# A decoder layer with latent attention, cross attention and routed experts: the router taken four sequences at a time, and the first loads, the turned x1 and the seam put in another order

## The chip, the core and the metric

The kernel runs on one core of a Trainium2 chip. A core has five engines that work at the same time, each with its own queue: TensorE (PE: matrix products and transposes; its weight loads are shown as PEld), VectorE (DVE), ScalarE (ACT), GpSimd (POOL) and SyncE (SP, which only issues DMAs here). The metric is the device time of one launch in microseconds (us); lower is better.

## What is computed

There are 32 sequences of 256 tokens with 256 features, and for each a context of 120 tokens. All data are float32. Cut to what matters:

```python
x = layernorm(x + latent_attention(x))        # causal, 16 heads, 72 latents
x = layernorm(x + cross_attention(x, ctx))    # 16 heads of 64
x = layernorm(x + experts(x))

def experts(h):                               # 16 experts of width 512
    scores = softmax(h @ gate_w.T).transpose(0, 2, 1)      # b, expert, token
    topk_w, topk_idx = top_k(scores, 32)      # each expert takes 32 tokens of each sequence
    x_tok = h[topk_idx]
    eo = (gelu(x_tok @ Wg.T) * (x_tok @ Wu.T)) @ Wd.T * topk_w
    return scatter_add(eo, topk_idx) + shared(h)           # shared: one gated layer for all
```

The router is the line with `scores`: a product of each token's 256 features with 16 columns, a softmax over the 16, and later the 32 best tokens of each expert.

## The kernel before

**Stages.** A first part does both attentions and the router, a second the experts. In the first part a loop runs over rounds n = 0 to 31, and each round holds work of three sequences: the latent attention of sequence n, the cross attention of n - 1, and the end of the cross attention and the router of n - 2. In the second part the sequences fall in two parts of 16; in each, 16 experts (`Expert`) gather their tokens by index, and 8 pairs of sequences (`Shared`) go through the shared layer and are stored.

**Order of work.** `tc.manual_schedule(engines={PE})` around both parts means that PE's instructions stand in the order in which the Python program writes them. The other engines' order is made by a planner, which takes by priority what its own clock holds for ready; `urgent()` raises a priority. Once made, the order on each queue is fixed, and an instruction that waits holds back all behind it on its engine. DMAs are issued by SP, except a few at the start by ACT and the gathers and scatters by index, which POOL issues.

**A round.** It has four sections, one for each group of four heads (`scores(n, g, k)`, then `turn` of the group before, then `queries` of the next). `queries(s, g)` (L330) multiplies by wd_sb and also fetches, with four small DMAs of SP (L334), the last 8 of the 72 latents of each head out of the tile q8, which `query_rest` (L317) has computed for all 16 heads at once. The tile qT has two buffers. `weigh` and `weigh_rest` (L461, products of 32 columns put into quarters of the array) use the softmax. `latent_out` adds and normalises to x1; `cross_values`, `turn_x1` (the tile x1T), `cross_queries`, `cross_scores`, `cross_turn`, `cross_weigh` and `cross_out` are the cross attention; `cross_out` ends in x2. A layernorm is DVE work with one POOL instruction in the middle (L150, the reciprocal root).

**The router.** `turn_x2` turns x2 and stores it for the shared layer. `route` (L622) makes, for one sequence, four products with the turned x2 as the stationary side and gate_w's 16 columns as the moving side, the softmax (two exponentials on ACT), a copy of the 16 scores behind the 256 features of x2 on POOL (L646), and two DMAs: the rows of 272 numbers that the experts gather, and the rows they add to. `select` (L651) ranks the tokens of eight sequences on DVE, and `place` (L680) makes the indices.

**PSUM.** Products land in a ring of six banks (tag "r") and two banks (tag "l", cross scores).

**The start.** `first_weights` (L217) loads wd_w straight into the two packed places of wd_sb: 64 latents of each head by two DMAs of SP, the last 8 of each head by two DMAs of ACT, and the biases by small DMAs (L233: 16 of them). `load_weights` and `out_weights` (18 DMAs) follow the first section of round 0 in the program.

**The seam.** After the rounds, `first_section(32)` still runs for the last two sequences. Then the rest of the last cross attention is written by hand between stretches of the first experts' work: `feed_forward` is a generator, and `fill(n)` takes n stretches of it. Its first stretch loads the weights and rows of units 0 and 1 and turns unit 0's. An expert's rows have three buffers (tag "xe"). A unit's stretches are four pairs of gate and up products, then two halves of its down product; then its rows are scattered, and unit u + 2 is loaded.

Of the kernel before, what the change touches and what calls it, by code (L numbers as in the profile page):

```python
# [26 lines left out]
P = 128  # L27
# [5 lines left out]
def decoder_kernel(  # L33
# [45 lines left out]
    LR = L - LM  # L79
    QSCALE = 1.0 / float(C // H) ** 0.5  # L80
# [59 lines left out]
    def layernorm(pool, dst, r, name):  # L140

        mv = pool.tile([P, TC, 2], F32, tag="mv", bufs=2, name=f"mv_{name}")
        rstd = pool.tile([P, TC], F32, tag="rstd", bufs=2, name=f"rstd_{name}")
        with urgent():
            for t in range(TC):
                st = pool.tile([P, 6], F32, tag="st", bufs=2, name=f"st_{name}_{t}")
                nc.vector.bn_stats(st, r[:, t, :])
                nc.vector.bn_aggr(mv[:, t, :], st)
            nc.vector.tensor_scalar(rstd, mv[:, :, 1], EPS, None, ALU.add)  # L149
            nc.gpsimd.tensor_tensor(rstd, rstd, mhalf, ALU.pow)  # L150
            for t in range(TC):
                nc.vector.tensor_scalar(
                    dst[:, t, :],
                    r[:, t, :],
                    mv[:, t, 0:1],
                    rstd[:, t : t + 1],
                    ALU.subtract,
                    ALU.mult,
                )
# [51 lines left out]
    gw_sb = cw.tile([P, DC, E], F32, name="gw_sb")  # L211

    v_bufs = [wp.tile([P, TC, VW], F32, name=f"v_{k}") for k in range(2)]
    for vb in v_bufs:
        nc.gpsimd.memset(vb, 0.0)

    def first_weights():  # L217
        nc.sync.dma_start(out=lat_sb, in_=latent_w.rearrange("(c p) l -> p c l", p=P))
        nc.sync.dma_start(out=latb, in_=latent_b.unsqueeze(1))
        by_head = wd_w.rearrange("(c p) (h l) -> p c h l", p=P, l=L)  # L220
        for d in range(DC):
            nc.scalar.dma_start(
                out=wd_sb[:, d, H * LM :].rearrange("p (h l) -> p h l", l=LR),
                in_=by_head[:, d, :, LM:],
            )
        for d in range(DC):
            nc.sync.dma_start(
                out=wd_sb[:, d, : H * LM].rearrange("p (h l) -> p h l", l=LM),
                in_=by_head[:, d, :, 0:LM],
            )  # L230
        nc.sync.dma_start(out=wdb_sb, in_=wd_b)
        for h in range(H):
            nc.scalar.dma_start(  # L233
                out=wdbs[h * LR : (h + 1) * LR, ZC - 1 : ZC], in_=wd_b[LM:, h : h + 1]
            )

        for odd in range(2):
            nc.vector.tensor_scalar(
                wdbs[odd * LM : (odd + 1) * LM, 0 : H // 2],
                wdb_sb[0:LM, :].rearrange("l (c two) -> l c two", two=2)[:, :, odd],  # L240
                QSCALE,
                None,
                ALU.mult,
            )
        nc.vector.tensor_scalar(
            wdbs[:, ZC - 1 : ZC], wdbs[:, ZC - 1 : ZC], QSCALE, None, ALU.mult
        )
        nc.sync.dma_start(out=outb, in_=out_b.partition_broadcast(P))
# [5 lines left out]
    def out_weights():  # L254
# [3 lines left out]
        for odd in range(2):  # L258
            nc.sync.dma_start(
                out=ow_sb[odd * LM : (odd + 1) * LM, 0 : ZC - 1, :], in_=by_pair[odd, 0:LM]  # L260
            )
        for h in range(H):
# [11 lines left out]
    def load(s):  # L274
# [3 lines left out]
        nc.sync.dma_start(out=st["x"], in_=x[s].rearrange("(t p) d -> p t d", p=P))  # L278
        st["c"] = ap.tile([P, DC, S2], F32, tag="c", bufs=3, name=f"c_{s}")
# [47 lines left out]
    def queries(s, g):  # L327
# [4 lines left out]
        for j in range(HG):  # L332
            h = g * HG + j
            nc.sync.dma_start(  # L334
                out=qT[LM:L, j, :], in_=st["q8"][h * LR : (h + 1) * LR, :]
# [264 lines left out]
    def cross_out(s):  # L600
# [10 lines left out]

        st["x2"] = ap.tile([P, TC, XW], F32, tag="x2", name=f"x2_{st['nm']}")
        layernorm(ap, st["x2"][:, :, 0:C], r2, f"2_{st['nm']}")

    def turn_x2(s):
        st = states[s]
        st["x2T"] = ap.tile([P, DC, T], F32, tag="xnT", bufs=1, name=f"x2T_{st['nm']}")
        transposed(st["x2T"], st["x2"][:, :, 0:C], f"px2T_{st['nm']}")
        nc.sync.dma_start(out=x2ts[s // 2][:, :, s % 2, :], in_=st["x2T"])

    def route(s):

        st = states[s]
        nm = st["nm"]
        pg = bank("r", [P, TC, E], f"pg_{nm}")
        for t in range(TC):
            project(
                pg[:, t, :],
                [(st["x2T"][:, d, t * P : (t + 1) * P], gw_sb[:, d, :]) for d in range(DC)],
            )  # L630
        gmax = ap.tile([P, TC], F32, tag="gmax", name=f"gmax_{nm}")
        nc.vector.tensor_reduce(gmax, pg, AX.X, ALU.max, negate=True)
        ge = ap.tile([P, TC, E], F32, tag="gexp", name=f"gexp_{nm}")
        gsum = ap.tile([P, TC, 1], F32, tag="gsum", name=f"gsum_{nm}")
        for t in range(TC):
            nc.scalar.activation(
                ge[:, t, :],
                pg[:, t, :],
                AF.Exp,
                bias=gmax[:, t : t + 1],  # L640
                accum_out=gsum[:, t, :],
            )
        nc.vector.reciprocal(gsum, gsum)
        score = scs[s // BG][:, :, s % BG, :]
        nc.vector.tensor_tensor(score, ge, gsum.to_broadcast([P, TC, E]), ALU.mult)
        nc.gpsimd.tensor_copy(st["x2"][:, :, C:], score)  # L646
        nc.sync.dma_start(
            out=xrows[s // BQ][block_rows(s), :].rearrange("(t p) d -> p t d", p=P), in_=st["x2"]
        )
        nc.sync.dma_start(  # L650
            out=acc[s // BQ][block_rows(s), :].rearrange("(t p) d -> p t d", p=P),  # L651
            in_=st["x2"][:, :, 0:C],
        )
        states[s] = {}
# [36 lines left out]
    ats = {}  # L691

# [4 lines left out]


    def first_section(n):
# [11 lines left out]
        run(weigh_rest, n - 1)  # L711
        run(cross_weigh, n - 2, 4)
        run(latent_out, n - 1)
        run(load, n + 1)
        run(cross_out, n - 2)
        run(cross_values, n - 1, 0)
        run(cross_values, n - 1, 1)
        run(turn_x1, n - 1)
# [8 lines left out]
    with tc.manual_schedule(engines={mybir.EngineType.PE}):  # L727
        load(0)
        first_weights()
        turn_x(0)  # L730
# [4 lines left out]
        for n in range(B):  # L735
            first_section(n)
            if n == 0:
                load_weights([(wk_sb, wk)])
                out_weights()
                load_weights([(wv_sb, wv), (wq_sb, wq), (wo_sb, wo), (gw_sb, gate_w)])  # L740

            run(scores, n, 1, 0)
            run(scores, n, 1, 1)
            run(turn, n, 0, 0)
            run(turn, n, 0, 1)
            run(scores, n, 1, 2)
            run(turn, n, 0, 2)
            run(queries, n, 2)
            run(cross_scores, n - 1, 0, 1)
            run(turn_x2, n - 2)  # L750
            run(cross_turn, n - 1, 0, 0, 0)
            run(cross_turn, n - 1, 0, 0, 1)
            run(cross_keys, n, 0)
            run(route, n - 2)

            run(scores, n, 2, 0)
            run(scores, n, 2, 1)
            run(turn, n, 1, 0)
            run(turn, n, 1, 1)
            run(scores, n, 2, 2)  # L760
            run(turn, n, 1, 2)
            run(cross_turn, n - 1, 0, 1, 0)
            run(queries, n, 3)
            run(cross_turn, n - 1, 0, 1, 1)
            run(turn_x, n + 1)
            run(weigh, n, 0)
            run(weigh, n, 1)
            run(cross_weigh, n - 1, 0)
            run(cross_scores, n - 1, 4, 0)
            run(keys, n + 1)  # L770
            run(query_rest, n + 1)

            run(scores, n, 3, 0)
            run(scores, n, 3, 1)
            run(turn, n, 2, 0)
            run(turn, n, 2, 1)
            run(scores, n, 3, 2)
            run(turn, n, 2, 2)
            run(values, n + 1)
            run(queries, n + 1, 0)  # L780
            run(cross_scores, n - 1, 4, 1)
            run(cross_turn, n - 1, 4, 0, 0)
            run(cross_turn, n - 1, 4, 0, 1)
            run(cross_keys, n, 1)


            if n - 2 >= BG and (n - 2) % BG == 0:
                place((n - 2) // BG - 1)
            if n - 2 >= 0 and (n - 1) % BG == 0:
                select((n - 2) // BG)  # L790
# [83 lines left out]
    class Shared:  # L874
# [27 lines left out]
        def down(self):  # L902
            for i, back in enumerate(self.backs):
# [7 lines left out]
                nc.vector.tensor_tensor(back, po, back, ALU.add)  # L911
                layernorm(fp, back, back, f"3_{s}")
                nc.sync.dma_start(out=out[s].rearrange("(t p) d -> p t d", p=P), in_=back)
# [17 lines left out]
    def feed_forward():  # L931
# [5 lines left out]
        units[0].load()  # L937
        units[1].load()
# [19 lines left out]
    with tc.manual_schedule(engines={mybir.EngineType.PE}):  # L958
# [3 lines left out]
        route(last - 1)  # L962
# [21 lines left out]
        route(last)  # L984
# [58 lines left out]
```

## Time and profile before

| what | us |
|---|---|
| median of three runs | 3546.3 (3544.41 to 3547.76) |
| the profiled execution | 3547.01 |
| its span, first to last instruction | 3545.2 |
| first scores of round 0 on PE | 21.98 |
| output product of latent attention, round by round | every 76.9 |
| last output product of latent attention, its start | 2457.26 |
| last product of the experts, its start | 3531.08 |

TensorE's granted clock is 0.996 of full speed over the span. In the timeline, times are from the span's start. A group of matmuls is given with its start, its length, its shapes (stationary, moving) and a count; a float32 product shows as two instructions, a transpose as one. A matmul's length includes the time in which it drains, which overlaps the next one, so the distance from start to start says what it costs.

### The profile page before, as it was taken

What the parts mean: (1) busy time and instruction counts of PE and PEld (TensorE: products, weight loads), DVE (VectorE), ACT (ScalarE), POOL (GpSimd) and SP (SyncE); (2) the same over time, 40 slices, a digit from 0 to 9 for tenths busy, and PEclk for the clock granted to TensorE, in tenths of its full rate; (3) what the DMA queues carried; (4) which work ended last, traced back from release to release, by engine and by line L of the source; (5) the groups of instructions that cost most, each with busy time, mean ns of one, the idle gap of its engine ahead of it and who ended that gap; (6) DMA issues with size and microseconds to landing.
All of it is one profiled execution on the core that took longest, in us unless ns stands there. A gap on an engine that the chain in (4) does not pass through costs nothing.

```text
span 3545.2 us, 58568 instructions
## 1 busy us (share of the span) xinstructions
PE 3480.9 (98%) x21580; PEld 2651.5 (75%) x21580; DVE 1627.3 (46%) x3674; ACT 1516.2 (43%) x5576; POOL 1092.4 (31%) x1100
## 2 busy tenths in 40 slices
PE   8999999999999999999999999998999999999999
PEld 6888888888888888888888888886655665555665
DVE  3555555565555556555455655544322223212233
ACT  3555554455555455555445555544411111111111
POOL 2233332223332223333222333223344420344310
PEclk9999999999999999999999999999999999999999
DMA  3000000000000000000000000001355542455421
GB/s 90 14 19 19 17 17 19 21 16 22 16 17 16 19 20 18 21 17 17 16 22 17 20 19 17 17 15 67 88 125 122 124 127 66 92 124 122 103 82 54
DMA packets 144198, 164.47 MB, mean 46 GB/s; under 512 B 31272, under 2 KB 120104, under 8 KB 143912
## 3 DMA queue, kind: packets, MB, share of 16 engines
q1 hardware_dynamic: 114952, 125.96, 11.9%
q0 software_dynamic: 24576, 34.62, 5.6%
q8 instruction: 172, 2.82, 0.3%
q14 instruction: 114, 0.93, 0.1%
q10 hardware_dynamic: 4384, 0.13, 0.1%
HBM read 105.61 MB, written 50.86 MB: 44 GB/s over the span
## 4 chain that ended last, share of the span: by engine, by line
PE 97%; DVE 1%; DMA 1%; POOL 1%; issue 0%; ACT 0%; ACTq 0%; POOLq 0%; DVEq 0%
PE po L176 13%; PE pS L375 10%; PE pq L176 7%; PE pg L176 7%; PE pqx L176 7%; PE pd L176 6%; PE pu L176 6%; PE pz L440 5%; PE pT L420 5%; PE pL L547 4%; PE pxT L570 3%; PE pc L586 3%; PE pkx L176 3%; PE pu_s L176 3%; PE pg_s L176 3%; PE pfo L176 3%
## 5 line engine op out<-in xcount | busy, mean ns | idle before, releaser
L402 POOL TENSOR_TENSOR sm<-sm,rs 128x512 f32<-128x512 f32 x384 | 396.6, 1040 | 357.4 <-DVE rs L401 334.5
L402 POOL TENSOR_TENSOR xsm_x<-xsm_x,rs_x 128x480 f32<-128x480 f32 x256 | 252.5, 986 | 729.4 <-DVE rs_x L401 727.5
L394 ACT ACTIVATE sm<-sm,nmax 128x128 f32<-128x128 f32 (+1 forms) x1024 | 458.5, 456 | 32.4 <-DVE nmax L388 30.8
L394 ACT ACTIVATE xsm_x<-pL,nmax_x 128x120 f32<-128x120 f32 x1024 | 359.6, 375 | 126.1 <-DVE nmax_x L557 124.9
L375 PE MATMUL pS<-kT,qT 72*128 72x128 f32 (+1 forms) x2048 | 388.1, 333 | 10.1 <-DMA qT<-q 9.3
L150 POOL TENSOR_TENSOR rstd<-rstd,mhalf 128x2 f32<-128x2 f32 x96 | 66.7, 695 | 908.2 <-DVE rstd L149 908.1
L375 PEld LDWEIGHTS pS<-kT,qT 72*128 72x128 f32 x2048 | 299.3, 194 | 29.3 <-issue 9.6
L384 DVE TENSOR_TENSOR sm<-pS,mask 128x512 f32<-128x512 f32 x384 | 261.6, 681 | 104.9 <-PE pS L375 101.2
L866 POOL DMA_INDIRECT acc<-eo,offs x128 | 200.3, 1565 | 341.2 <-DVE eo L861 300.6
L176 PE MATMUL pq<-xT,wd_sb 128*128 128x256 f32 x1152 | 281.4, 385 | 1.9 <-DMA wd_sb<-in_wd_w_dram 1.9
L176 PE MATMUL pqx<-x1T,wq_sb 128*128 128x256 f32 x1024 | 240.3, 388 | 33.1 <-DVE x1T L170 33.1
L516 ACT COPY vx<-pvx 120x512 f32<-120x512 f32 x64 | 37.5, 586 | 541.3 <-PE pvx L176 541.3
L388 DVE TENSOR_REDUCE nmax<-sm 128x2 f32<-128x512 f32 (+1 forms) x384 | 257.6, 671 | 1.4
L176 PE MATMUL po<-ow_sb,zT 128*128 128x256 f32 x1152 | 257.2, 382 | 0.0
L176 PEld LDWEIGHTS po<-ow_sb,zT 128*128 128x128 f32 x1152 | 216.3, 190 | 40.2 <-DVE cxT L598 11.2
L928 DVE TENSOR_TENSOR hT<-gl,pu 128x512 f32<-128x512 f32 x128 | 87.9, 687 | 339.6 <-PE pu L176 258.4
L176 PEld LDWEIGHTS pqx<-x1T,wq_sb 128*128 128x128 f32 x1024 | 190.8, 191 | 68.0 <-DVE x1T L170 40.6
L176 PE MATMUL pg<-xeT,wg 128*128 128x512 f32 x512 | 240.8, 593 | 0.8 <-DVE xeT L842 0.8
L176 PE MATMUL pu<-xeT,wu 128*128 128x512 f32 x512 | 240.6, 592 | 0.0
L176 PEld LDWEIGHTS pq<-xT,wd_sb 128*128 128x128 f32 x1152 | 211.6, 193 | 29.0 <-DMA wd_sb<-in_wd_w_dram 3.3
L176 PE MATMUL pd<-wd,hT 128*128 128x256 f32 x1024 | 226.6, 379 | 0.0
L176 PE MATMUL po<-wo_sb,cxT 128*128 128x256 f32 x1024 | 226.2, 379 | 0.0
(123 smaller groups left out, 5900.7 us busy)
## 6 DMA issues: line engine op xcount, KB each, us to landing
wg<-in_wg_dram SPq DMA_DIRECT2D x32, 512.0 KB
wu<-in_wu_dram SPq DMA_DIRECT2D x32, 512.0 KB
wd<-in_wd_dram SPq DMA_DIRECT2D x32, 512.0 KB
rows<-x SPq DMA_DIRECT2D x32, 272.0 KB
x<-in_x_dram SPq DMA_DIRECT2D x32, 256.0 KB
qT<-q SPq DMA_DIRECT2D x512, 8.0 KB
acc<-x SPq DMA_DIRECT2D x32, 256.0 KB
x2t<-x2T SPq DMA_DIRECT2D x32, 256.0 KB
```

The costliest lines, as they stand in the source:

```text
L176: nc.tensor.matmul(acc, lhsT, rhs, start=(i == 0), stop=(i == n - 1))
L375: nc.tensor.matmul(pS[:, a, :], st["qT", g][:, j, t * P : (t + 1) * P], st["kT"][:, 0:width], start=True, stop=True,)
L384: nc.vector.tensor_tensor(sm, pS, m.unsqueeze(1).to_broadcast([P, n, width]), ALU.add)
L388: nc.vector.tensor_reduce(nmax, sm, AX.X, ALU.max, negate=True)
L394: nc.scalar.activation(dst[:, a, :], src[:, a, :], AF.Exp, bias=nmax[:, a : a + 1], accum_out=rs[:, a, :],)
L402: nc.gpsimd.tensor_tensor(dst, dst, rs.to_broadcast([P, n, width]), ALU.mult)
L420: nc.tensor.transpose(pT[:, j, :], block, ident)
L440: nc.tensor.matmul(pz[odd * LM : (odd + 1) * LM, a, k * P :], st["v"][:, k, 0:LM], moving(st, g, 2 * a + odd, k), start=(k == 0), stop=(k ...
L547: nc.tensor.matmul(pLs[odd][:, j, :], st["qxT", c0][rows, j, t * P : (t + 1) * P], st["kxT"][rows, c0 + j, :], start=True, stop=True,)
L570: nc.tensor.transpose(pT[:, j, :], st["xsm", c0, t, odd][:, j, :], ident)
L586: nc.tensor.matmul(pc[odd * DH : (odd + 1) * DH, a, :], st["vx"][:, 2 * (c0 + j0 + a) + odd, :], st["xpt", c0, odd][:, j0 + a, :], start=True,
L866: nc.gpsimd.indirect_dma_start(out=acc[b], out_offset=self.rows(b), in_=eo[:, k, :], in_offset=None, compute_op=ALU.add,)
```

## The change

Six edits, all in one step.

- **Router.** gate_w is kept with 32 columns, the upper 16 zero. The turned x2 of four sequences is collected in one tile x2T (one buffer). In rounds 6, 10, ... 30, `route(b)` multiplies with gate_w stationary and the turned x2 moving: each sequence has a quarter of the array's columns and of the 128 result partitions. DVE copies the result, `score(b)` turns it back with two transposes and does the softmax for four sequences: one exponential on ACT, more on DVE. The scores go straight from their tile to the last 16 columns of the rows with two DMAs. x2's own rows are stored by `cross_out`. `route` stands behind `weigh_rest` in the first section, `score` behind the second `cross_values`. Ranking and placing come one round later; block 7 is routed and scored at the seam.
- **x1.** `turn_x1` stands between the two halves of `cross_values` instead of behind both.
- **First loads.** wd_w comes as one contiguous DMA into ow_sb's place, and DVE (the last 8 latents, group 0) and POOL (groups 1 to 3) copy it into wd_sb. The last 8 latents are laid out with the head inside, so q8's rows of one head lie 16 partitions apart. The biases' small DMAs are one. In the preamble and round 0 SP's order is as written too: the first qT group before the second sequence, wk and the rest, out_w in two halves between the later groups.
- **Seam.** `feed_forward` yields after unit 0's load. The rest of `first_section(32)` (from cross_out on) is inside the hand-written seam, after that one stretch, and POOL's order is as written from there to the end of the kernel.
- **End.** The last sequence is added, normalised and stored in two halves of 128 tokens.
- `load` is split in two (x, context).

```diff
     def queries(s, g):
             nc.sync.dma_start(
-                out=qT[LM:L, j, :], in_=st["q8"][h * LR : (h + 1) * LR, :]
+                out=qT[LM:L, j, :], in_=st["q8"][h::H, :]
             )
...
     def first_weights():
+        raw = ow_sb.rearrange("p a b -> p (a b)").rearrange("p (c n) -> p c n", c=DC)
         nc.sync.dma_start(out=lat_sb, in_=latent_w.rearrange("(c p) l -> p c l", p=P))
-        nc.sync.dma_start(out=latb, in_=latent_b.unsqueeze(1))
+        nc.sync.dma_start(out=raw, in_=wd_w.rearrange("(c p) n -> p c n", p=P))
+        nc.scalar.dma_start(out=latb, in_=latent_b.unsqueeze(1))
+        nc.scalar.dma_start(
+            out=wdbs[:, ZC - 1 : ZC], in_=wd_b[LM:, :].rearrange("l h -> (l h)").unsqueeze(1)
+        )
+        nc.scalar.dma_start(out=wdb_sb, in_=wd_b)
+        by_head = raw.rearrange("p c (h l) -> p c h l", l=L)
+        def pack(copy, g):
+            at = slice(2 * g * P, 2 * (g + 1) * P)
+            copy(
+                wd_sb[:, :, at].rearrange("p c (h l) -> p c h l", l=LM),
+                by_head[:, :, g * HG : (g + 1) * HG, 0:LM],
+            )
         for d in range(DC):
-            nc.scalar.dma_start(
...
+            nc.vector.tensor_copy(
+                wd_sb[:, d, H * LM :].rearrange("p (l h) -> p l h", h=H),
+                by_head[:, d, :, LM:].rearrange("p h l -> p l h"),
+            )
...
+        pack(nc.vector.tensor_copy, 0)
...
+        for g in range(1, NG):
+            pack(nc.gpsimd.tensor_copy, g)
...
+    def route(b):
+        pg = bank("r", [P, T], f"pg_{b}")
+        for d in range(DC):
+            for i in range(BQ):
+                nc.tensor.matmul(
+                    pg[i * QW : (i + 1) * QW, :],
+                    gw_sb[:, d, :],
+                    blocks[b][:, d, i, :],
+                    start=(d == 0),
+                    stop=(d == DC - 1),
+                )
+        gT = ap.tile([P, T], F32, tag="gT", bufs=1, name=f"gT_{b}")
+        with urgent():
+            nc.vector.tensor_copy(gT, pg)
+        blocks[b] = gT
+
+    def score(b):
+        pg = bank("r", [P, TC * BQ, QW], f"pgT_{b}")
+        gT = blocks.pop(b)
         for t in range(TC):
...
+            nc.tensor.transpose(
+                pg[:, t * BQ : (t + 1) * BQ, :].rearrange("p i e -> p (i e)"),
+                gT[:, t * P : (t + 1) * P],
+                ident,
+            )
...
+        nc.scalar.activation(ge, ge, AF.Exp)
...
+            rows = xrows[b][:, C:].rearrange("(i t p) e -> t p i e", t=TC, p=P)
+            nc.sync.dma_start(out=rows[t], in_=sc)
...
+    def routed(n):
+        return 3 <= n < B and (n - 2) % BQ == 0
...
         run(weigh_rest, n - 1)
+        if routed(n):
+            route((n - 3) // BQ)
         run(cross_weigh, n - 2, 4)
         run(latent_out, n - 1)
-        run(load, n + 1)
+    def first_section_rest(n):
+        if n:
+            run(load, n + 1)
+            run(load_context, n + 1)
         run(cross_out, n - 2)
         run(cross_values, n - 1, 0)
+        run(turn_x1, n - 1)
         run(cross_values, n - 1, 1)
-        run(turn_x1, n - 1)
+        if routed(n):
+            score((n - 3) // BQ)
...
+    with tc.manual_schedule(engines={mybir.EngineType.PE, mybir.EngineType.SP}):
         load(0)
         first_weights()
+        load_context(0)
...
+        load(1)
+        load_context(1)
+        load_weights([(wk_sb, wk)])
+        attention_round(0)
+    with tc.manual_schedule(engines={mybir.EngineType.PE}):
+        for n in range(1, B):
+            attention_round(n)
         first_section(B)
...
         units[0].load()
+        yield
         units[1].load()
         units[0].turn()
         yield
...
-    with tc.manual_schedule(engines={mybir.EngineType.PE}):
+    with tc.manual_schedule(engines={mybir.EngineType.PE, mybir.EngineType.Pool}):
+        fill(1)
+        first_section_rest(B)
         cross_scores(last, 0, 1)
         turn_x2(last - 1)
         fill(2)
-        route(last - 1)
...
         turn_x2(last)
         fill(1)
-        route(last)
+        route(last // BQ)
+        fill(1)
+        score(last // BQ)
         fill(3)
```

## The prediction

> **What bounds the kernel now.** I read the page first (busy shares, the chain that ended last), then TensorE's own waits, then the timeline where those waits sit.
>
> ```profile
> PE 3480.9 (98%) x21580; PEld 2651.5 (75%) x21580; DVE 1627.3 (46%) x3674; ACT 1516.2 (43%) x5576; POOL 1092.4 (31%) x1100
> ...
> PE 97%; DVE 1%; DMA 1%; POOL 1%; issue 0%; ACT 0%; ACTq 0%; POOLq 0%; DVEq 0%
> ```
>
> TensorE (PE) is the chain. Time can only come from PE work removed, from PE's waits, and from stretches in which PE runs slowly. The waits of PE, in total us, times, longest:
>
> ```profile
> PE pqx L176 <- DVE x1T L170: 33.1, 32, 8.8
> PE pS L375 <- DMA qT<-q: 9.3, 2, 6.3
> PE pxT L570 <- POOL xsm_x L402: 4.2, 2, 2.3
> ```
>
> One short wait in each of 31 rounds, one long one at the seam between attention and experts, two at the start: these are the places of the change.
>
> **The router.** Timeline of PE; start, us, what:
>
> ```profile
> 142.92 2.81 PE L461 MATMUL pzr<-pt,v 128*32 128x256 f32 x64
> 145.66 1.95 PE L586 MATMUL pc<-xpt,vx 120*64 120x256 f32 x16
> ...
> 185.42 0.97 PE L176 MATMUL pg<-gw_sb,x2T 128*128 128x16 f32 x8
> 186.24 2.00 PE L375 MATMUL pS<-kT,qT 72*128 72x128 f32 x12
> 188.08 1.04 PE L420 MATMUL pT<-ident,sm 128*128 128x128 f32 x8
> ```
>
> Starts count, not durations (an end contains the drain). Routing one sequence: 186.24 - 185.42 = 0.82, and the scores behind it take 1.84 where the same twelve without a router in front take 1.76 (200.74 to 202.50): 0.90 each, 32 x 0.90 = 28.8 us. The new form has 16 passes of 32 columns by 256 for four sequences. Its nearest row is pzr, also 32 columns in four quarters: 64 passes, half of 256 and half of 128, in 145.66 - 142.92 = 2.74 us, so 2.74/48 = 0.057 per 256 and 0.91 for 16. The two score transposes cost 0.11 each (pT: eight in 0.88); I add 0.1 for the seams between forms. 8 x 1.23 = 9.8 us: **gain 19**. Bounds: if the quarters did not overlap, 16 x 0.215 (pq: eight of 256 in 1.72) makes 29.3 and a gain of -0.5; with no seams 20. I take the pzr row. Off PE, the route's copy has latent_out, cross_out and the values (over 16 us) before score needs it; score's reductions have until its bank comes round again, six banks later. 64-byte score rows, two DMAs a block, stand on SP between the context load and the next qT group (166.46 and 179.16: 12 us free), and nothing reads them before the experts. Without that gap one round in four would lose their issue, nearest row gw_sb's 2.53 us: at most 2 x 2.5 x 8 = 40. x2's two row stores only move up to where one of them stands already (165.99). The next block's x2T waits for route to have read the old one, which is a whole section earlier. Ranking and placing come a round later; their users are the experts.
>
> **The wait for x1T.** All engines of one round:
>
> ```profile
> 165.22 0.74 DVE L152 TENSOR_SCALAR x<-r,mv,rstd 128x256 f32<-128x256 f32 x2 [0.80 <-POOL rstd L150]
> ...
> 166.39 0.69 DVE L170 COPY x1T<-px1T 128x512 f32<-128x512 f32 x1 [0.43 <-PE px1T L166]
> ...
> 167.13 5.23 PE L176 MATMUL pqx<-x1T,wq_sb 128*128 128x256 f32 x23 [0.78 <-DVE x1T L170]
> ```
>
> The transposes begin at 165.75 and issue for 4 x 0.11, so PE could go on at 166.19 and goes on at 167.13: 0.94 lost. With one value half (1.72) behind them, px1T is ready at 166.39 - 1.72 = 164.67, x1 itself has been there since 159.06, and PE comes to the queries at 166.19 as before. What is late next is the DVE queue: between 164.42 and 165.22 it idles for POOL's rstd of x2, then normalises x2 until 165.96. If the copy stands in that gap, it ends at 165.4 and nothing is left of the wait; if it stands behind the normalisation, it ends about 166.65, the queries start at 166.67, and 0.48 is left. The order on DVE isn't in this trace. Ends 0.46 and 0.94 a round; by readiness in this trace the copy is first by half a microsecond, too little to trust a planner's clock, so I take 0.70: 31 x 0.70 = **22** (14 to 29).
>
> **The start.** Chain of waits, then SP's own waits:
>
> ```profile
> 14.98 6.86 DMA qT<-q
> ...
> 37.51 8.25 DMA qT<-q
> SPq L334 <- DMA wo_sb<-in_wo_dram: 3.1, 1, 3.1
> ```
>
> The first scores wait until 21.98 and the third group's until 45.90, because qT's small copies stand on SP behind weights: a DMA issue waits for an older one to finish, 18 out_w issues take 23.77 to 33.4, the four big loads follow. After the change wd_w comes as one contiguous load third on SP, issued about 2.2; x needed 3.9 to arrive, and 1.18 MB at the 300 to 416 GB/s of the densest slices takes 2.8 to 3.9 more: about 7.3. Two small DVE copies (0.25 each by the 0.21 to 0.29 of the v copies) lead to query_rest: four slow passes of 0.43, ACT 0.46, q8 near 10.3, against 14.96. Four qT issues at 0.62 and two to three us of landing: first scores near 15, saving 7. Behind them on SP come load 1, wk (used at 40.95) and the second qT group, then a half of out_w (used near 68) between the later groups; no qT group waits for a big load that is less than a group old. The packs on POOL (three of about 1 us, by the 1.04 of a 512-wide product) are through by 12, before the second queries. From the first scores to the end of the first key block before took 42.7 - 21.98 = 20.7, at a slow clock for most of it (pq eight in 3.43 against 1.72). I keep these 20.7: third scores at 35.7 instead of 45.9. The next group was then slow again until 52 (5.66 of work in 8.55), which no longer happens: 2.9. **Gain 13.** Here a rule stands against the row: the Trainium skill, "TensorE: Matmul & The Clock Gate", Part 1, has the array at full clock after about 3.4 us of activity and cold again after such a window of idleness. By it the scores would be warm soon after 18 and the 11.7 us of full-speed work between (2.62 + 1.72 + 2.62 + 1.32 + 1.72 + 1.74) would end near 30: gain 19. But the trace, broken by small waits, is slow until 38.5, so I take the row. Ends 7 (only the DMA order helps at one place) and 19.
>
> **The seam.** Timeline of all engines:
>
> ```profile
> 2482.73 0.73 POOL L150 TENSOR_TENSOR rstd<-rstd,mhalf 128x2 f32<-128x2 f32 x1
> 2483.49 0.73 DVE L152 TENSOR_SCALAR x<-r,mv,rstd 128x256 f32<-128x256 f32 x2 [9.36 <-POOL rstd L150]
> 2484.14 0.68 DVE L170 COPY x1T<-px1T 128x512 f32<-128x512 f32 x1
> ```
>
> The x1T copy is behind x2's normalisation on DVE, that behind rstd on POOL, and that behind gathers for three experts at 1.25 us each; mv was ready at 2474.1. PE starts again at 2484.88 instead of 2475.91, and the 24 query passes take 7.59 where a round shows 5.45. By hand only the first expert's four gathers go ahead; they follow rstd of x1 at 2467.3 and end at 2473, so rstd of x2 isn't held. The second expert's four stand behind the products of the second cross scores (2501.3 to 2503.6) and land by 2512, wanted at 2523; the next products on POOL are due at 2510. At most 0.5 is left, as in a round: 8.97 + 2.14 - 0.5 = 10.6. **What is late next:** POOL in written order puts rstd of the last x2, ready at 2542.1, ahead of expert 0's scatter, and unit 2's gathers after that. Scatter 7.5 us, four gathers 1.25 to 1.3 apart, 2.8 to land: the last rows at 2557.3, wanted at about 2555.9. That costs 1.4, no more clock. Seam: **gain 9** (5 to 11). The 5 us of waits at 2440 to 2448 are untouched.
>
> **The end.** The last sequence is added, normalised and stored in halves: one 256-wide chain instead of a 512-wide one (0.3 + 0.37 + 0.15 + 0.37 shorter) and half the store, unless the first half delays the second on DVE: 0 to 1.2, **0.7**.
>
> **Sum** against the profiled execution (3547.0, span 3545.2 plus 1.8): 19 + 22 + 13 + 9 + 0.7 = 63.7, so 3483.3; the median is 0.7 below the profiled one: 3483. Removed exponentials and POOL's score copy cover nothing and gain nothing.
>
> **Rivals.**
> Slower: the experts' gathers. Before, POOL issued 12 gathers before any scatter, a unit ahead; in written order those for unit u+2 come after scatter u. In a steady unit: scatter from 2646.72, gathers at 2654.20 to 2658.06, landing 2.8, so 2660.9, wanted at 2662.95: 2.0 us of slack, 30 units. Each us beyond costs 30; the change is slower from 2.0 + 63.7/30 = 4.1 us extra per unit (5 us would give 3573). Against it: the median landing is 2.8 with the same scatters ahead of it; for it, the longest was 6.4. Chance 0.05, a fifth of it within the 0.2% below.
> Small gain: x1T behind x2's normalisation (14), start only 7, seam 6, or quarters that drain against each other (router 10): 14 + 15 + 7 + 6 = 42, 3505. For it: only the written order of PE is certain. Chance 0.23.
> Large gain: copy in the gap (29), start by the rule (19), seam 11, router 20: 79, 3468. Chance 0.20.
> The forecast, 3474 to 3494: 0.51. The router not overlapping at all, 3503: 0.01.
>
> 0.2% (7 us) is about what a measurement of this kernel can tell from no change. Range 3464 to 3507. Faster 0.95, same 0.01, slower 0.04.
>
> **What would show it.** Right: one route of about 0.9 us per four sequences; pqx's wait under 0.5 in a round; first scores near 15 and third near 36; no 8.8 at the seam, a wait of 1 to 2 for the third expert's rows. Wrong: px waiting for gathers in every unit, pS waiting for qT inside rounds (its source rows now lie 16 partitions apart; slack about 3 us), a cold PE after 40 us.

## The result, and the profile after

| | before | after |
|---|---|---|
| median, us | 3545.8 (4 runs, 3544.41 to 3547.76) | 3494.85 (4 runs, 3492.36 to 3495.5) |
| ratio, 95% interval | | 0.9855 (0.9837 to 0.9872) |
| the profiled execution / its span | 3547.01 / 3545.2 | 3492.36 / 3490.2 |
| first scores on PE | 21.98 | 19.13 |
| third scores | 45.90 | 37.73 |
| first output product of latent attention | 78.61 | 67.34 |
| last one | 2457.26 | 2409.66 |
| last product of the experts | 3531.08 | 3475.89 |

The change saves 51.0 us between the medians and 55.0 between the two spans; the profiled execution of after was its fastest. The forecast was 63.7 between spans. The rows of the table cut the 55.0 into places: 11.3 before the first latent output product, 36.3 in the 31 rounds to the last one, 7.6 between that one and the last product of the experts, and -0.2 behind it.

The page of after, busy shares and the chain that ended last:

```profile
PE 3449.6 (99%) x21468; PEld 2617.0 (75%) x21468; DVE 1632.7 (47%) x3639; ACT 1499.0 (43%) x5456; POOL 1090.3 (31%) x1073
...
PE 94%; DVE 3%; issue 1%; POOL 1%; DMA 1%; SPq 0%; ACT 0%; POOLq 0%; DVEq 0%; ACTq 0%
```

PE is still the chain, and its busy time fell by 31.3. TensorE's waits in after (total us, times, longest):

```profile
PE pk L178 <- DVE xT L172: 7.4, 1, 7.4
PE pqx L178 <- DVE x1T L172: 6.3, 24, 0.3
PE pxT L585 <- POOL xsm_x L417: 4.2, 2, 2.3
PE pxT L168 <- DMA x<-in_x_dram: 4.0, 1, 4.0
PE px L898 <- DMA xe<-rows,offs: 2.9, 2, 2.6
PE pS L390 <- DMA qT<-q: 2.3, 1, 2.3
PE px1T L168 <- DVE x L154: 1.6, 1, 1.6
```

The 33.1 us of waits for x1T are 6.3, the 8.8 at the seam is gone, and qT costs 2.3 rather than 9.3. One wait has grown: the first keys wait 7.4 for xT, where before it was 0.8. Two are new: the third expert's transposes wait 2.9 for gathered rows, and in round 1 the transposes of x1 wait 1.6 for x1, since no cross_out stands ahead of them there.

A plain round in after, all engines (start, length, engine, line, operation):

```profile
153.44 0.60 PE L168 MATMUL px1T<-ident,x 128*128 128x128 f32 x4
...
154.62 0.74 DVE L154 TENSOR_SCALAR x<-r,mv,rstd 128x256 f32<-128x256 f32 x2 [0.80 <-POOL rstd L152]
...
155.27 0.69 DVE L172 COPY x1T<-px1T 128x512 f32<-128x512 f32 x1
...
156.01 2.21 PE L178 MATMUL pqx<-x1T,wq_sb 128*128 128x256 f32 x9 [0.26 <-DVE x1T L172]
```

The transposes are through by 154.1, DVE is idle for 0.80 while POOL makes rstd for x2, and yet the copy stands behind x2's normalisation. It was ready in time and queued too late.

A round with a router, PE only:

```profile
434.40 2.81 PE L476 MATMUL pzr<-pt,v 128*32 128x256 f32 x64
437.03 1.05 PE L650 MATMUL pg<-x2T,gw_sb 128*32 128x256 f32 x16
438.00 1.95 PE L601 MATMUL pc<-xpt,vx 120*64 120x256 f32 x16
...
458.53 0.38 PE L667 MATMUL pgT<-ident,gT 128*128 128x128 f32 x2
458.96 1.35 PE L178 MATMUL pqx<-x1T,wq_sb 128*128 128x256 f32 x5
```

Start to start, the router of four sequences takes 0.97. The two transposes of score stand where PE would otherwise wait for x1T, so here they cost nothing: from one latent output product to the next it is 76.38 with a router in between and 75.52 without, 0.86 apart. (The experiment a2 below has no such wait, and there the transposes add 0.22 to the stretch behind.)

The start in after, all engines:

```profile
9.77 0.88 DVE L242 COPY wd_sb<-ow_sb 128x128 f32<-128x128 f32 x2 [1.26 <-DMA ow_sb<-in_wd_w_dram]
...
10.57 0.84 DVE L236 COPY wd_sb<-ow_sb 128x512 f32<-128x512 f32 x1
...
11.77 0.68 DVE L172 COPY xT<-pxT 128x512 f32<-128x512 f32 x1
...
12.50 1.98 PE L178 MATMUL pk<-xT,lat_sb 128*72 128x256 f32 x4 [7.38 <-DVE xT L172]
...
16.72 2.58 SPq L349 DMA_DIRECT2D qT<-q  x4
...
19.13 0.49 PE L390 MATMUL pS<-kT,qT 72*128 72x128 f32 x2 [0.43 <-ACT qT L363]
```

The copy of the turned x needs only PE's four transposes of x, which begin at 4.04 and have ended by 5.13, but it stands on DVE behind the copies into wd_sb, the first of which waits for wd_w until 9.77. So the keys start at 12.50, and q8 is fetched from 16.72: later than before, not sooner.

### The profile page after: what moved, and what is told of

It is laid out like the page before. It is cut to its first block, busy times and chain, and to the rows that moved or that the text cites. A ratio compares the mean times of both kernels' runs of the same rounds, so it can differ in the third digit from the quotient of the medians.

```text
span 3490.2 us, 58138 instructions
## 1 busy us (share of the span) xinstructions
PE 3449.6 (99%) x21468; PEld 2617.0 (75%) x21468; DVE 1632.7 (47%) x3639; ACT 1499.0 (43%) x5456; POOL 1090.3 (31%) x1073
## 4 chain that ended last, share of the span: by engine, by line
PE 94%; DVE 3%; issue 1%; POOL 1%; DMA 1%; SPq 0%; ACT 0%; POOLq 0%; DVEq 0%; ACTq 0%
PE po L178 13%; PE pS L390 10%; PE pq L178 7%; PE pqx L178 7%; PE pd L178 6%; PE pg L178 6%; PE pu L178 6%; PE pz L455 5%; PE pT L435 5%; PE pL L562 4%; PE pxT L585 3%; PE pc L601 3%; PE pkx L178 3%; PE pu_s L178 3%; PE pg_s L178 3%; PE pfo L178 3%
## 5 line engine op out<-in xcount | busy, mean ns | idle before, releaser
L390 PE MATMUL pS<-kT,qT 72*128 72x128 f32 (+1 forms) x2048 | 380.4, 329 | 3.3 <-DMA qT<-q 2.3
L152 POOL TENSOR_TENSOR rstd<-rstd,mhalf 128x2 f32<-128x2 f32 (+1 forms) x97 | 67.2, 693 | 935.4 <-DVE rstd L151 935.4
```

The costliest lines, as they stand in the source:

```text
L390: nc.tensor.matmul(pS[:, a, :], st["qT", g][:, j, t * P : (t + 1) * P], st["kT"][:, 0:width], start=True, stop=True,)
```

## The experiments

Each kernel is after with the edit shown, unless said otherwise; differences are between medians, against 3494.85 for after. Beside the experiments before measured 3546.42 to 3546.7, beside after 3545.83, so a difference of 1 us says nothing.

**Both value halves ahead of x1's transposes (a1).**

```diff
         run(cross_values, n - 1, 0)
-        run(turn_x1, n - 1)
         run(cross_values, n - 1, 1)
+        run(turn_x1, n - 1)
```

> The changed kernel with turn_x1 behind both halves of the values, as before. If the split of the values is what shortened the wait, each of 30 rounds loses 0.94 on PE again instead of 0.41, less about 0.4 in the 7 rounds where score's transposes lie in the wait: 14 to 17 us slower than the changed kernel. Rival (the rounds became shorter by the router alone): no difference beyond 3 us.

Measured: 3509.98 (3507.36 to 3510.87), 15.1 slower than after. The wait is back:

```profile
PE pqx L178 <- DVE x1T L172: 23.6, 32, 0.8
```

So this part of the change is worth about 15 us: a plain round is 76.04, 0.52 longer, and the 31 rounds together take 16.6 more.

**x1T copied by ACT (a2).**

```diff
-        transposed(st["x1T"], st["x1"], f"px1T_{st['nm']}")
+        transposed(st["x1T"], st["x1"], f"px1T_{st['nm']}", nc.scalar.copy)
```

> The changed kernel with the copy of x1T out of PSUM on ACT instead of DVE. Theory: what is left of the wait (0.41 a round) is the place of the copy on DVE behind x2's normalisation. ACT has only the values' copies there, so the wait should vanish in all rounds: about 24 x 0.41 = 10 us faster than the changed kernel, PE's list without pqx. Rival (the transposes themselves come too late, or x1 is late): the wait stays and the time with it, within 2 us.

Measured: 3479.05 (3478.43 to 3480.7), 15.8 faster than after; a plain round is 74.99. All engines of the same stretch:

```profile
153.55 1.88 PE L178 MATMUL pvx<-wv_sb,c 128*120 128x512 f32 x4
...
153.80 0.59 ACT L172 COPY x1T<-px1T 128x512 f32<-128x512 f32 x1
154.30 0.74 DVE L154 TENSOR_SCALAR x<-r,mv,rstd 128x256 f32<-128x256 f32 x2 [0.80 <-POOL rstd L152]
...
155.27 2.97 PE L178 MATMUL pqx<-x1T,wq_sb 128*128 128x256 f32 x13
```

With the copy on an engine whose queue is free, the queries follow the second value half without a wait. The direction was expected, the size missed: I had reckoned 0.41 a round, from start to start, and nothing in routed rounds. A plain round gains 0.53; the seven stretches behind a router gain 0.31, because the transposes of score, which the wait had hidden, now show. That is 13.5 over the 31 rounds; the profiled spans lie 12.9 apart, the medians 15.8 (after's profile is its fastest execution). In plain rounds, a1, after and a2 together show a wait of 1.05, of which the change takes one half and the copy on ACT the other.

**One router per sequence again (a3).** `route(s)` as it was in before (products with the turned x2 stationary), with all other parts of the change kept.

> The changed kernel with the router's product and softmax per sequence again (16 moving columns, at its old place in the round and at the seam), all else as changed. Theory: 0.90 a sequence against about 0.95 for four, so 28.8 - 7.6 = 21 us slower than the changed kernel, and 2 to 3 more because score's transposes no longer lie inside pqx's wait in 7 rounds. Rival (the quarters run one behind the other, so the new form costs the same): within 3 us.

Measured: 3516.55 (3513.2 to 3517.38), 21.7 slower. A round is 76.42 long. A plain one of after is 75.52, so one sequence's router costs 0.90, as the timeline of before had said; four in quarters cost 0.86 together. The 2 to 3 us more that I expected for the transposes of score did not show.

**xT first on DVE (a4).** DVE's order, too, as written in the preamble, with turn_x(0) and keys(0) ahead of the copies that wait for wd_w.

```diff
-    with tc.manual_schedule(engines={mybir.EngineType.PE, mybir.EngineType.SP}):
+    with tc.manual_schedule(
+        engines={mybir.EngineType.PE, mybir.EngineType.SP, mybir.EngineType.DVE}
+    ):
         load(0)
         first_weights()
         load_context(0)
-        turn_x(0)
-        keys(0)
+    with tc.manual_schedule(engines={mybir.EngineType.PE, mybir.EngineType.SP}):
         query_rest(0)
...
     def first_weights():
...
+        turn_x(0)
+        keys(0)
         by_head = raw.rearrange("p c (h l) -> p c h l", l=L)
```

> The changed kernel with DVE's order at the very start as written: the copy of xT ahead of the copies that wait for wd_w. Theory: keys and query_rest waited for xT until 12.5 only because that copy stood behind them on DVE; now keys are done before wd_w lands at 9.7, q8 is ready near 13 instead of 16.7, first scores near 16: 3 to 4 us faster than the changed kernel. Rival (wd_w's landing and the slow clock alone set the start): under 1 us.

Measured: 3490.6 (3488.52 to 3492.83), 4.3 faster than after. PE in a4:

```profile
5.87 1.98 PE L178 MATMUL pk<-xT,lat_sb 128*72 128x256 f32 x4 [0.79 <-DVE xT L172]
...
14.92 0.49 PE L392 MATMUL pS<-kT,qT 72*128 72x128 f32 x2 [0.43 <-ACT qT L365]
```

The keys start at 5.87 instead of 12.50, q8 is fetched from 12.26, and the first scores are at 14.92.

**SP's order by the planner (b3).**

```diff
-    with tc.manual_schedule(engines={mybir.EngineType.PE, mybir.EngineType.SP}):
+    with tc.manual_schedule(engines={mybir.EngineType.PE}):
```

> The changed kernel with SP's order in the preamble and round 0 left to the planner: the second sequence's x and context, wk and half of out_w ahead of the first qT group. Theory: 1.4 MB more compete with wd_w's load, and the first q8 comes later by their transfer: 3 to 5 us slower than the changed kernel, first scores near 22 instead of 19. Rival (with the one contiguous load, SP's order no longer matters): within 1 us.

Measured: 3493.35 (3491.74 to 3495.39), no different from after. The theory that SP's hand-written order brings the start's gain fell: first scores at 18.89, and the first latent output product even 2.3 earlier (65.02).

**Weights written where they stood before (c1).** As b3, and wk, out_w, wv, wq, wo and gate_w again between the first section of round 0 and the rest, loads of the next sequence ahead of them as before. wd_w stays one contiguous load.

> The changed kernel with SP's order left to the planner and the weight loads written where they stood before, all behind round 0's first section; wd_w still comes as one load. Theory: with the hand order gone the start lost nothing (b3), so the gain at the start comes from where out_w and the big loads are written; here the third qT group stands behind all of them again, the third scores begin at 43 or later instead of 35 to 38: 6 to 9 us slower than the changed kernel. Rival (the one contiguous load of wd_w is the gain): within 2 us.

Measured: 3502.26 (3501.62 to 3503.42), 7.4 slower than after. SP's timeline in c1:

```profile
24.94 4.96 SPq L276 DMA_DIRECT2D ow_sb<-in_out_w_dram  x8
29.94 0.40 SPq L265 DMA_DIRECT2D wv_sb<-in_wv_dram  x1
...
32.01 2.02 SPq L265 DMA_DIRECT2D gw_sb<-in_gate_w_dram  x1
34.15 8.08 SPq L349 DMA_DIRECT2D qT<-q  x8
```

and PE's in the same kernel:

```profile
41.66 3.75 PE L390 MATMUL pS<-kT,qT 72*128 72x128 f32 x12 [8.20 <-DMA qT<-q]
```

The third group's qT stands behind out_w and the big loads again. PE waits 8.20 for it (before waited 3.0 at this place, because its PE came there later), the third scores begin at 41.66 instead of 37.73, and they take 3.75 instead of 1.93, at a granted clock of 0.50. Against b3, which has the same planner's order on SP, the time is 8.9 longer. So where the weights stand in the program is what gains at the start.

**The old small loads in the new order (c2).** wd_w in two packed pieces by SP and two by ACT, the biases one by one, q8 with a head's 8 rows side by side; SP's order as in after.

> The changed kernel with wd_w and the biases loaded as before, straight into their places (4096 pieces of 256 bytes and 4096 of 32, 16 small bias loads), q8's rows of a head side by side; SP's hand order stays. Theory: before, q8 was ready at 14.96, now at 16.7, so the one load gains nothing: within 2 us of the changed kernel, first scores near 19. Rival: 4 us or more slower.

Measured: 3494.69 (3493.89 to 3495.47): no difference. PE in c2:

```profile
13.40 2.62 PE L178 MATMUL pq<-xT,wd_sb 128*128 128x256 f32 x6 [2.85 <-DMA wd_sb<-in_wd_w_dram]
```

In after, the contiguous load gains nothing: part of the query passes wait for wd_w until 13.40 in c2, and in after the xT copy keeps all of them until 14.28. But c2 belongs beside a4 too. Both have their keys early (at 5.60 and 5.87); with the small loads the first scores are at 18.10, with the contiguous one at 14.92, and the medians are 4.1 apart. So the contiguous load gains once the xT copy is out of its way. The rows 16 partitions apart cost nothing in the rounds: a plain one is 75.52 in c2 as in after.

**POOL's order at the seam by the planner (b1).**

```diff
-    with tc.manual_schedule(engines={mybir.EngineType.PE, mybir.EngineType.Pool}):
+    with tc.manual_schedule(engines={mybir.EngineType.PE}):
```

> The changed kernel with POOL's order at the seam left to the planner, which puts eight more gathers ahead of rstd of the second last x2 and all later gathers a unit ahead. Theory: rstd waits 8 x 1.25 = 10 us more, x1T behind it, so PE waits about 9 at the seam and runs cold for the queries after it (2), while the wait for the third expert's rows (3.4) goes: 6 to 9 us slower than the changed kernel. Rival (the seam's gain came from the stretches' new order alone): within 2 us.

Measured: 3500.68 (3497.23 to 3501.1), 5.8 slower (the spans of the profiled executions: 9.0). All engines in b1:

```profile
2435.33 0.95 POOL L889 DMA_INDIRECT xe<-rows,offs  x1 [0.30 <-issue]
2436.29 0.74 POOL L152 TENSOR_TENSOR rstd<-rstd,mhalf 128x2 f32<-128x2 f32 x1
2437.06 0.73 DVE L154 TENSOR_SCALAR x<-r,mv,rstd 128x256 f32<-128x256 f32 x2 [9.36 <-POOL rstd L152]
2437.71 0.68 DVE L172 COPY x1T<-px1T 128x512 f32<-128x512 f32 x1
...
2438.45 7.90 PE L178 MATMUL pqx<-x1T,wq_sb 128*128 128x256 f32 x24 [8.83 <-DVE x1T L172]
```

The gathers of three experts stand ahead of rstd again, the x1T copy behind both, and the 24 query passes run at a granted clock of 0.68. The same place in after:

```profile
2427.40 0.73 DVE L154 TENSOR_SCALAR x<-r,mv,rstd 128x256 f32<-128x256 f32 x2 [0.85 <-POOL rstd L152]
2428.05 0.68 DVE L172 COPY x1T<-px1T 128x512 f32<-128x512 f32 x1
...
2428.79 3.50 PE L178 MATMUL pqx<-x1T,wq_sb 128*128 128x256 f32 x15 [0.31 <-DVE x1T L172]
```

**The gathers of unit u + 2 ahead of unit u's scatter (b2).** `Expert.load` is split: `fetch()` issues the gathers.

```diff
         units[0].load()
+        units[0].fetch()
...
                 units[u + 1].turn()
+            if u + 2 < len(units):
+                units[u + 2].fetch()
             yield
```

> The changed kernel with the gathers of unit u + 2 written ahead of unit u's down product, so ahead of its scatter on POOL. Theory: the one wait of PE for gathered rows (2.9 us of waits, 3.4 from start to start) goes and nothing else changes: 3 us faster than the changed kernel. Rival (every unit lost something to the late gathers): 10 us or more.

Measured: 3488.96 (3488.13 to 3489.35), 5.9 faster than after; between the profiled spans 3.3 (3486.9 against 3490.2). The wait for the third expert's rows is gone. Of after, POOL and PE at this place (first POOL's timeline, a scatter of unit 0 and the last gather of unit 2; then PE's):

```profile
2484.00 1.78 POOL L929 DMA_INDIRECT acc<-eo,offs  x1 [0.20 <-issue]
...
2495.53 0.95 POOL L889 DMA_INDIRECT xe<-rows,offs  x1 [0.30 <-issue]
```

```profile
2497.38 0.33 PE L898 MATMUL px<-ident,xe 128*128 128x128 f32 x1 [0.28 <-DMA xe<-rows,offs]
2500.33 0.77 PE L898 MATMUL px<-ident,xe 128*128 128x128 f32 x5 [2.63 <-DMA xe<-rows,offs]
```

The last gather is issued at 2495.53 and its rows are used at 2500.33, 4.8 later; the two waits sum to 2.9, and against the same transposes without a wait the place is 3.4 longer. The rest of the 5.9 isn't explained by a row: the runs of after lie 3.1 apart, and its profile is the fastest of them. In c3, which is like after at this place, the wait of 2.43 is followed by a slow stretch that after's profile does not have (last section). The other executions of after may have had one; they left no trace.

**The last sequence stored whole (c3, a single run).** `parts = [slice(0, TC)]` for every sequence.

> The changed kernel with the last sequence stored whole. From the start of the last product to the end of the span it was 14.12 before and 14.31 changed. Theory: the halves stand one behind the other on DVE and give nothing: 14.1 to 14.2. Rival: 14.8 or more.

Measured: 3495.17, span 3492.7. From the last product of the experts to the end of the span it takes 14.1, with halves 14.3, before 14.1. The halves gain nothing: both halves' additions stand on DVE at 3482.99, behind the normalisation of the sequence ahead.

**The repairs together (b4).** a2, a4 and b2, and in the last first_section the softmax's use (`weigh`, `weigh_rest`) ahead of the two cross_turns that wait there for POOL.

> Four edits together on the changed kernel: x1T's copy on ACT, xT's copy first on DVE, gathers ahead of the scatter, and in the last first_section weigh and weigh_rest ahead of the two cross_turns that wait for POOL. If the parts add up: 15.8 + 4.2 + 3 and 4 to 6 for the last, about 3467. If they cover one another: above 3475.

Measured: 3463.85 (3462.08 to 3466.3), ratio to before 0.9769 (0.9756 to 0.9782): 31.0 faster than after, faster than both kernels. The chain that ended last in b4:

```profile
PE 99%; DVE 0%; ACT 0%; DMA 0%; POOL 0%; issue 0%; POOLq 0%; SPq 0%; ACTq 0%; DVEq 0%
```

a2, a4 and b2 gave 15.8 + 4.3 + 5.9 = 26.0, so about 5 are left for the last section, whose two waits of together 4.2 on POOL's products are gone. That edit was not run alone; the 5 is a difference of medians.

**b4 with SP's order by the planner (c4).**

> The four edits of b4 and SP's order left to the planner. Theory: in b3 the planner's order had the first output product 2.2 earlier (65.09 against 67.34), lost again at the seam by chance of the profile: 0 to 2 us faster than b4, about 3462. Rival (the hand order is worth something once q8 comes earlier): 2 us or more slower than b4.

Measured: 3470.38 (3467.86 to 3470.88), 6.5 slower than b4. SP's timeline in c4:

```profile
13.27 0.76 SPq L273 DMA_DIRECT2D ow_sb<-in_out_w_dram  x1
14.14 5.00 SPq L351 DMA_DIRECT2D qT<-q  x8
```

and PE's:

```profile
18.85 5.46 PE L392 MATMUL pS<-kT,qT 72*128 72x128 f32 x16 [3.25 <-DMA qT<-q]
```

In b4 the first scores start at 15.56. Here a part of out_w goes ahead of qT just when q8 is ready (qT is issued at 12.19 in b4), and PE waits 3.25. The sixteen passes then take 5.46, and the granted clock is 0.50 from 20 to 34, where b4 has 0.86 from 20 to 26 and 1.00 behind; why the slow stretch is longer here isn't shown. My expectation missed. In b3 the same part of out_w goes at 11.76, and q8 is ready only for a fetch at 16.57, so there it holds up nothing. Once DVE's order is mended, SP's hand order is worth 6.5.

## Why the prediction was right, and where its sizes were off

The measured median is inside the range of 3464 to 3507, and 0.9 above the middle band of 3474 to 3494. Router, x1T, start and seam moved for the reasons given, the end did not move. The forecast was too high by 8.7 between spans (63.7 against 55.0), and the medians make 3.2 more of it: the profiled execution was 0.7 above the median that the prediction had for before and is 2.5 below that of after. One sum on record does not come out: the small gain's rival puts the router at 15 where its text says 10; with 10 it is 37 and not 42.

- **Router: 19 forecast, 22 measured.** 32 x 0.90 less 8 x 0.86 is 21.9, and a3 gives 21.7; about 21 of it lies in the rounds and 1 at the seam. The row of pzr (0.91 for 16 passes) was the right price. The 0.22 of the transposes lies in the remaining wait for x1T (without that wait, in a2, it shows), and the 0.1 for seams did not appear. The quarters overlap (0.06 a pass where one behind the other would take 0.215), so the rival without a gain is out.
- **x1T: 22 forecast, 16 measured.** This is the term that was mis-sized. The prediction gave two ends, the copy in DVE's gap or behind x2's normalisation, and "so I take 0.70", their middle. A queue order has one value: the copy stands behind the normalisation in every round, the end that it priced at 0.46 and that is worth 0.52 (a1). The 0.53 left over is the other half of the wait (a2).
- **Start: 13 forecast, 10.6 measured** (11.3 less the 0.7 that round 1 loses by its wait of 1.6). The third scores came near the forecast (37.73 for 35.7), with the weights no longer ahead of qT as the reason given (c1), but in part by luck: see below. The first scores didn't (19.13 for 15): wd_w landed at 9.7 rather than "about 7.3", and the copies into wd_sb hold DVE's queue ahead of the xT copy, which the sum had not asked for, so that "q8 near 10.3" became 16.7. a4, which mends the order alone, has the first scores at 14.92. The contiguous load, from which the prediction started, gains nothing in after (c2), and neither does SP's hand order (b3); both gain once DVE's order is mended (a4 against c2, b4 against c4).
- **Seam: 9 forecast, 6.6 measured** (7.6 less the 1 that is the router's). The wait of 8.8 went for the reason given (b1 brings it back). What comes late next was named, the third expert's rows, but it costs 3.4 and not "1.4": the last gather took 4.8 from issue to use, where the median landing of 2.8 had been put in.
- **End: 0.7 forecast, -0.2 measured.** The two halves stand one behind the other on DVE, and storing the last sequence whole is no slower (c3).
- The slower rival, gathers late in every unit, was wrong: only the third expert waits (two waits, 2.9), and the order with the gathers ahead (b2) gains 3.3 to 5.9 in all, no 30 units.

Between the row of before and the rule of the Trainium skill that was weighed against it ("TensorE: Matmul & The Clock Gate", Part 1), the row was nearer: third scores at 37.73, by the row 35.7, by the rule near 30. But two errors cancelled in part: the first scores came 4.1 late, and the third followed them after 18.6 and not 20.7. And at first the passes ran as the rule has it: eight query passes take 1.89 from 22.72 on, warm, where before's took 3.43. What held the third scores back after that were a wait of 2.26 for the second qT group and a slow stretch (last section), and neither was in the sum.

## What to carry to other kernels

When a product or a load is moved so that its input is ready sooner, look at the queue of the engine that copies it: what counts is what stands ahead of the copy and what that waits for. Where the order of that queue isn't known, price both orders and choose one, or move the copy to an engine whose queue is free; don't average. An edit that shows no gain can be masked by a second wait that ends later (SP's order here), so try it again once that one is mended.

## What the runs showed of the hardware

**A short wait costs more than PE's idle row says.** In a plain round of after, the idle time shown is 0.26. Another 0.15 is the drain of the last value product, which otherwise overlaps (four passes are 1.88 long and cost 1.72), and 0.11 comes because the first weight load has waited as well: the 24 query passes take 5.45, in a2 5.34. That makes 0.52, and the round is 0.53 longer.

**At the start the granted clock does not tell how fast the passes run.** PE at the start of after, in two cuts:

```profile
14.28 3.19 PE L178 MATMUL pq<-xT,wd_sb 128*128 128x256 f32 x7
17.26 1.31 PE L178 MATMUL pq<-xT,wd_sb 128*128 128x256 f32 x5
```

From 14.28 to 17.26 seven passes take 0.43 each, twice the 0.215 of a warm one, while the profile gives a clock of 1.00 from 12.40 to 17.40. From 17.26 to 18.41 five take 0.23 each. The keys had begun at 12.50, so the array became fast about 5 us into unbroken work.

**Waits of two to three us were sometimes followed by a slow stretch, and sometimes not.** Stretches of after, a2, c3 and again after (from:to, length, busy time of each engine with its instructions, granted clock, DMA share, GB/s):

```profile
26.00:34.00 8.00, 7.13 (x29) 6.23 (x30) 4.71 (x9) 3.35 (x15) 2.04 (x2) 0.60 0.39 77
20.00:26.00 6.00, 5.40 (x19) 4.49 (x19) 3.93 (x8) 1.68 (x9) 0.00 (x0) 0.66 0.77 246
2501.50:2505.50 4.00, 4.00 (x14) 3.35 (x15) 3.53 (x12) 0.58 (x1) 0.00 (x0) 0.57 0.19 75
2500.30:2504.30 4.00, 3.97 (x21) 3.58 (x22) 3.42 (x11) 0.59 (x1) 0.00 (x0) 1.00 0.15 58
```

The first stretch lies behind after's wait of 2.26 (24.61 to 26.87). That wait need not be the cause: a2 has a slow stretch at the same age of the kernel, and from its first keys at 12.32 on PE has waited there 0.60 at most. The third and fourth lie behind the wait for the third expert's rows: c3 waited 2.43 and is slow, after waited 2.63 and is not. The Trainium skill ("TensorE: Matmul & The Clock Gate", Part 1) names a window of about 3.4 us of idleness for the fall of the clock; here it fell behind shorter waits too. What decides is not shown by these runs.
